# State space layer of a four-layer decoder: order of its first unit, one square root for two norms

## The chip, the cores and the metric

The kernel runs on one core of a Trainium2 chip. Its time is device microseconds from launch to end of one execution. Three runs of the kernel before are given with their median; one further execution was profiled, and it has a time of its own. Engines are called by their names or, in tables and profile lines, PE (TensorE's matmuls), PEld (its weight loads), DVE (VectorE), ACT (ScalarE), POOL (GpSimd) and SP (the sync engine, which issues DMAs).

## The reference, cut to what matters

The program is a decoder of four layers on 16 sequences of 128 tokens of width 256. Each layer adds an attention or state space part, a cross attention and an MLP to x, each on a layer norm of x. The change lies in layer 2's first part, a state space model that runs forward (`f`) and backward (`b`) over a sequence. The layer norm stands outside it and an RMS norm inside:

```
h   = (x - mean) / sqrt(var + eps)              # layer norm of x
xn  = rmsnorm(h, norm_w)                        # h * rsqrt(mean(h*h) + eps) * norm_w
z, xBC, dt = split(xn @ in_w.T)                 # 512 + 768 + 8 columns, per direction
dt  = softplus(dt + dt_bias)
xBC = silu(conv(xBC) + conv_b)                  # four taps over time, per channel
y   = ssd(xs, dt, -exp(A_log), B, C) + xs * D   # scan in chunks of 128 tokens
y   = rmsnorm(y * silu(z), gnorm_w) @ out_w.T
x   = x + h + concat(y_f, y_b) @ out_w_blk.T + out_b_blk
```

Since mean(h) is 0, mean(h*h) is var / (var + eps). So both norms of a token come from one variance.

## The kernel before, in words

All of x stays on the core as four groups `x[0]` to `x[3]` of four sequences each (128 partitions are the tokens of one sequence, 4 x 256 columns). Layers are written one after the other. A tile framework orders most instructions on each engine's queue; those given to `keep_in_program_order` (`pin`, and `pinned`, `pinned_transpose`) stay among themselves, on each engine, in the order in which the code issues them. Each engine takes its queue in order. Where two instructions touch one buffer, the later waits for the earlier through a semaphore.

PSUM buffers come from two pools: `b1` (one bank, 128x512 float32, four of them in rotation) and `b2` (two banks, two in rotation). A tile waits until the readers of the one that had its buffer before are through.

The layer before in time is layer 1's MLP (`l1_ffn`). It runs in 16 steps, one per sequence. ScalarE does per step a gate (L1217, silu), a rounding (L1253) and two evacuations of transposes (`yT`, L1235); VectorE a product (L1222), a maximum (L1091), small operations and the addition to x (L1245). Once a group of x is complete, the next layer's row operations on it can start in between.

`l2_attn` (L1266) does the following, in the order of the code:

- Weights are loaded and scaled, constants made, among them `na` (L1289, an exponential).
- `tokens(g)` (L1316 to L1338) makes the rows of one group: `bn_stats` and `bn_aggr` (L1323, L1324) for mean and variance; `rsqrt` (L190: a ScalarE square root, L191, and a VectorE reciprocal, L192) for `rs`; the normalised rows `h` (L1327, four operations); `ss` from var and `rs` (L1332, L1333) and a second `rsqrt`; x plus h (L1335); h scaled by `ss` on ScalarE (L1337, four operations); and `hidden_T`, eight TensorE transposes into two b1 tiles `tr` (L183), whose copies `hT` go to VectorE (L110) and ScalarE (L112) by turns. These transposes are not pinned.
- A `Unit` is one group in one direction; there are eight. For it `channel(u, ch)` computes 128 of the 768 columns of xBC for 512 tokens: two products into a b1 tile `xBC`, a ScalarE scaling (the last tap with bias), three VectorE taps (`stt`) that read the same b1 tile, all into `xs`. `silu(u, ch)` is applied in place by ScalarE, `gate(u, c)` makes 128 columns of z with its silu. ScalarE's operations of these have the line L1342, VectorE's L1346.
- The code before issues `tokens(0)`, then for each of six channels the channel and at once its silu, then four gates, then `tokens(1)` to `tokens(3)`.
- dt's chain follows (L1541 to L1575). Eight narrow products per all four groups go to one b1 tile, ScalarE copies it (`dT`, L1546), four transposes turn it (`dtt`), VectorE adds the bias (L1555), ScalarE does Abs, Exp and, later, Ln (L1561, L1562, L1568), and VectorE the rest, ending with `da` = A * dt (L1572, L1575).
- `sums(u)` takes cumulative sums of `da` on TensorE (`cs`), and VectorE and GpSimd make `left` and `right` from them.
- `pw` (L1577 on) is the product of both output projections, 16 products in 8 b1 tiles, each read by VectorE (L1584).
- The loop over eight units starts with `decays` of unit 0, whose first products go to two b2 tiles `seg`. In the loop, each unit's channels, gates and sums are issued one unit ahead, beside the work of the unit before it.

Functions that use a different activation table on ScalarE (square root, silu, Exp, Ln) have an ACT_TABLE_LOAD in front of them wherever the table changes.

Of the kernel before, what the change touches and what calls it, by code (L numbers as in the profile page):

```python
# [8 lines left out]
F = mybir.dt.float32  # L9
BF = mybir.dt.bfloat16  # L10
U32 = mybir.dt.uint32
AF = mybir.ActivationFunctionType
ALU = mybir.AluOpType
# [3 lines left out]
P = 128  # L17
# [4 lines left out]
NG = 4  # L22
GB = B // NG
GT = GB * P
EPS = 1e-5
# [4 lines left out]
class Decoder:  # L30
# [1235 lines left out]
    def l2_attn(self):  # L1266


        nc = self.nc
# [12 lines left out]
        with self.tc.tile_pool(name="l2a", bufs=1) as wk:  # L1282
# [28 lines left out]
            for i, d in enumerate(dirs):  # L1311
                nc.gpsimd.tensor_copy(wdt[:, :, NH * i : NH * i + NH], wx[d][:, :, CH : CH + NH])

            hTs = []

            def tokens(g):  # L1316

                h = self.hp.tile([P, GB, DM], F, tag="h", name="h", bufs=2)
                st = self.small([P, GB, 6], "bnst")
                mv = self.small([P, GB, 2], "bnmv")  # L1320
                rs = self.small([P, GB], "rstd")
                for t in range(GB):
                    nc.vector.bn_stats(st[:, t, :], self.x[g][:, t, :])  # L1323
                    nc.vector.bn_aggr(mv[:, t, :], st[:, t, :])  # L1324
                self.rsqrt(rs, mv[:, :, 1])
                for t in range(GB):
                    nc.vector.tensor_scalar(  # L1327
                        h[:, t, :], self.x[g][:, t, :], mv[:, t, 0:1], rs[:, t : t + 1], ALU.subtract, ALU.mult
                    )

                ss = self.small([P, GB], "ss")
                nc.vector.tensor_tensor(ss, mv[:, :, 1], rs, ALU.mult)  # L1332
                nc.vector.tensor_tensor(ss, ss, rs, ALU.mult)  # L1333
                self.rsqrt(ss, ss)
                nc.vector.tensor_tensor(self.x[g], self.x[g], h, ALU.add)  # L1335
                for t in range(GB):
                    nc.scalar.activation(h[:, t, :], h[:, t, :], AF.Copy, scale=ss[:, t : t + 1])  # L1337
                hTs.append(self.hidden_T(h))  # L1338


            pin = self.tc.keep_in_program_order
# [15 lines left out]
            def channel(u, ch):  # L1357

                ps = self.b1("xBC")
                for k in range(2):  # L1360
                    self.pinned(ps, wx[u.d][:, k, ch * P : (ch + 1) * P], hTs[u.g][:, k, :], start=k == 0, stop=k == 1)
                x = u.xs[:, ch, :]
                cw, cbias = self.c(f"L2_{u.d}_conv_w"), self.c(f"L2_{u.d}_conv_b")
                w = lambda k: cw[:, ch * 4 + k : ch * 4 + k + 1]
                act(x, ps, AF.Identity, scale=w(3), bias=cbias[:, ch : ch + 1])
                x3, p3 = (v.rearrange("p (t n) -> p t n", t=GB) for v in (x, ps))
                for n in range(1, 4):
                    late, early = slice(n, P), slice(0, P - n)
                    dst, src = (late, early) if u.d == "f" else (early, late)
                    stt(x3[:, :, dst], p3[:, :, src], w(3 - n), x3[:, :, dst], ALU.mult, ALU.add)  # L1370

            def silu(u, ch):
                act(u.xs[:, ch, :], u.xs[:, ch, :], AF.Silu)

            def gate(u, c):
                ps = self.b1("z")
                for k in range(2):
                    self.pinned(ps, wz[u.d][:, k, S(c)], hTs[u.g][:, k, :], start=k == 0, stop=k == 1)
                act(u.z[:, c, :], ps, AF.Silu)

            def sums(u):

                ps = self.b1("cs")[:, 0:P]
                for t in range(GB):
                    self.pinned(ps[R(t), :], da[:, u.i, u.g * GB + t, :], upto[u.d], start=True, stop=True)
                u.left = wk.tile([P, P], F, tag="left", name="left", bufs=2)
                cs = wk.tile([P, P], F, tag="cs", name="cs", bufs=2)
                u.right = wk.tile([P, NH, P], F, tag="right", name="right", bufs=1)
                yield
                ts(u.left, ps, kind[:, 1:2], kind[:, 0:1], ALU.mult, ALU.add)  # L1390
                ts(cs, ps, kind[:, 0:1], kind[:, 1:2], ALU.mult, ALU.add)
                nc.gpsimd.tensor_tensor(
                    u.right,
                    cs.unsqueeze(1).to_broadcast([P, NH, P]),
                    each.unsqueeze(2).to_broadcast([P, NH, P]),
                    ALU.mult,
                )
                yield
# [129 lines left out]
                stt(x, ps, u.rs[:, t : t + 1], x, ALU.mult, ALU.add)  # L1528


            tokens(0)
            u = Unit(0)
            for ch in (4, 5, 0, 1, 2, 3):
                channel(u, ch)
                silu(u, ch)
            for c in range(4):
                gate(u, c)
            for g in range(1, NG):
                tokens(g)

            ps = self.b1("dt")  # L1541
            for g in range(NG):
                for k in range(2):
                    self.pinned(ps[R(g), :], wdt[:, k, :], hTs[g][:, k, :], start=k == 0, stop=k == 1)
            dT = wk.tile([P, GT], F, tag="sq", name="dT", bufs=2)
            nc.scalar.copy(dT, ps)  # L1546
            ps = self.b1("dtt")
            for t in range(GB):
                self.pinned_transpose(ps[:, S(t)], dT[:, S(t)])

            dt = wk.tile([P, 2, B, NH], F, tag="dt", name="dt")
# [19 lines left out]
            for i in range(2):  # L1571
                nc.vector.tensor_tensor(  # L1572
                    da[:, i, :, 0:NH], dt[:, i], na[:, i, :].unsqueeze(1).to_broadcast([P, B, NH]), ALU.mult
                )
                nc.vector.tensor_scalar(da[:, i, :, NH : 2 * NH], da[:, i, :, 0:NH], -1.0, None, ALU.mult)  # L1575
            for _ in sums(u):
                pass  # L1577

            pw = wk.tile([P, 2, 4, DM], F, tag="pw", name="pw")
            for i, d in enumerate(dirs):  # L1580
                for c in range(4):
                    ps = self.b1("pw")[:, 0:DM]
# [5 lines left out]
            for m in range(M):  # L1588
# [56 lines left out]
                last, u = u, after  # L1645
# [765 lines left out]
```

## Time and profile before

| what | value |
|---|---|
| three runs | 3664.17, 3664.07, 3657.71 us; median 3664.07 |
| the profiled execution | 3659.25 us, its span 3657.5 us |
| mean granted TensorE clock | 0.949 |
| PE, DVE, ACT, POOL busy, share of the span | 91%, 58%, 39%, 12% |
| first xBC product starts | 1716.30 us |
| first `dt` product starts | 1751.68 us |
| `cs` starts | 1763.84 us |
| first `pw` product starts | 1764.42 us |
| first `seg` product starts | 1773.07 us |
| TensorE busy from 1716 to 1773 us | 35.43 of 57 us |
| VectorE, ScalarE busy there | 30.63 and 27.01 us |

A line of a timeline gives start, duration, engine, line of the code, operation, output and inputs with their shapes, how many instructions were merged, and in brackets how long the engine had stood before it and what it waited for last. A line of the busy table gives a stretch, its length, then busy time and number of instructions of PE, PEld, DVE, ACT and POOL, TensorE's granted clock, the DMA engines' busy share and GB/s. A duration of a merged line runs to the end of the last instruction; neighbours on TensorE overlap, so starts are the better measure of its pace.

### The profile page before, as it was taken

The numbers are of one execution on the slowest core, as the hardware profiler recorded it, in microseconds if no ns is written. First come the engines' busy times: TensorE is split into PE (matmuls) and PEld (weight loads), VectorE is DVE, ScalarE is ACT, GpSimd is POOL, SyncE is SP. The second block draws the span as 40 slices with busy tenths as digits, with TensorE's granted clock in tenths as the row PEclk, the third lists the DMA queues.
The fourth block names the chain that finished last, engine by engine and source line by source line (L and its number), as shares of the span: only waits on it lengthen the run. The fifth ranks groups of instructions, "written<-read, shape, count | busy, mean of one in ns | idle before, by whom it ended". The sixth has DMA issues, their size and how long they took to land.

```text
span 3657.5 us, 51423 instructions
## 1 busy us (share of the span) xinstructions
PE 3343.9 (91%) x20959; PEld 1806.8 (49%) x20976; DVE 2115.8 (58%) x4133; ACT 1426.7 (39%) x1917; POOL 457.2 (12%) x627
## 2 busy tenths in 40 slices
PE   7888999999998899997799999196999999999999
PEld 4655555555556556664455567062122222224656
DVE  6545444444463534468677644425799999973440
ACT  2344411111124422238455422023477777783221
POOL 5423100000003311110010110104100000002100
PEclk9978999999999999999999999597799999999989
DMA  3000000000110100010000001273312020000000
GB/s 98 4 7 1 14 20 20 18 22 18 32 48 2 38 1 1 1 42 8 12 1 12 2 1 34 105 250 107 60 25 31 11 31 11 11 1 25 1 8 18
DMA packets 90484, 105.46 MB, mean 29 GB/s; under 512 B 11364, under 2 KB 72678, under 8 KB 89990
## 3 DMA queue, kind: packets, MB, share of 16 engines
q1 hardware_dynamic: 79672, 89.71, 9.3%
q0 software_dynamic: 4224, 6.43, 0.5%
q10 hardware_dynamic: 6352, 6.03, 0.5%
q8 instruction: 165, 2.70, 0.3%
q14 instruction: 71, 0.58, 0.1%
HBM read 85.53 MB, written 16.60 MB: 28 GB/s over the span
## 4 chain that ended last, share of the span: by engine, by line
PE 79%; DVE 10%; ACT 5%; issue 3%; POOL 2%; DMA 1%; SPq 0%; POOLq 0%; ACTq 0%; DVEq 0%
PE acc L1943 7%; PE down L255 6%; PE gate L255 6%; PE up L255 6%; PE proj L255 6%; PE st L1943 5%; PE one L1943 4%; PE qT L166 4%; PE st L255 4%; PE o L255 2%; PE h L255 2%; DVE mx L2089 2%; PE rb L255 2%; PE v L948 2%; PE pr L166 2%
## 5 line engine op out<-in xcount | busy, mean ns | idle before, releaser
L2089 DVE TENSOR_REDUCE mx<-one 128x1 f32<-128x512 f32 x1024 | 659.0, 686 | 61.8 <-PE one L1943 52.7
L2226 ACT ACTIVATE e<-st 128x1024 f32<-128x1024 f32 x512 | 497.0, 1021 | 214.1 <-PE st L1943 213.0
L674 ACT ACTIVATE gs<-gate,cols 128x512 f32<-128x512 f32 x132 | 90.7, 687 | 552.6 <-PE gate L255 552.6
L1943 PE MATMUL acc<-e,v 128*32 128x512 f32 x2048 | 288.9, 613 | 0.9 <-ACT e L2226 0.9
L1943 PE MATMUL st<-qp,kp 113*128 113x512 bf16 x1024 | 273.8, 388 | 3.4 <-ACT e L2226 1.9
L688 DVE SCALAR_TENSOR_TENSOR x<-down,w_all,x 128x256 f32<-128x256 f32 x512 | 212.4, 477 | 111.1 <-PE down L255 110.9
L255 PE MATMUL down<-expert,gs 128*128 128x256 f32 x1056 | 251.0, 381 | 2.2 <-DVE gs L675 2.2
L255 PE MATMUL gate<-hT,expert 128*128 128x512 f32 x528 | 250.3, 596 | 0.0
L255 PE MATMUL up<-hT,expert 128*128 128x512 f32 x528 | 248.7, 593 | 0.0
L255 PEld LDWEIGHTS down<-expert,gs 128*128 128x128 f32 x1056 | 201.5, 191 | 86.1 <-issue 61.5
L675 DVE SCALAR_TENSOR_TENSOR gs<-up,cols,gs 128x512 f32<-128x512 f32 x132 | 99.0, 750 | 229.8 <-PE up L255 229.8
L1943 PE MATMUL one<-kp,qp 16*128 16x512 bf16 x1024 | 211.7, 399 | 4.0 <-DVE mx L2089 2.6
L1943 PEld LDWEIGHTS <-qp 16*128 16x128 bf16 x1024 | 49.0, 91 | 332.4 <-issue 327.0
L255 PEld LDWEIGHTS up<-hT,expert 128*128 128x128 f32 x528 | 100.8, 191 | 127.1 <-issue 126.9
L1943 PEld LDWEIGHTS <-kp 113*128 113x128 bf16 x1024 | 79.1, 98 | 141.8 <-issue 81.8
L1048 ACT COPY rb<-rb 128x512 f32<-128x512 f32 x64 | 37.5, 586 | 258.9 <-PE rb L255 258.9
L255 PEld LDWEIGHTS gate<-hT,expert 128*128 128x128 f32 x528 | 100.4, 192 | 70.5 <-issue 64.0
L1050 DVE TENSOR_TENSOR cT<-o,rb 128x512 f32<-128x512 f32 x64 | 44.3, 692 | 157.0 <-ACT rb L1048 157.0
L166 PE MATMUL qT<-hT,L_xattn_Wq 128*128 128x512 f32 x256 | 115.8, 606 | 6.6 <-DVE hT L110 4.5
L1346 DVE SCALAR_TENSOR_TENSOR xs<-xBC,cols,xs 128x508 f32<-128x508 f32 x144 | 106.1, 742 | 22.4 <-ACT xs L1342 19.0
L255 PE MATMUL o<-e,v 128*32 128x128 f32 (+1 forms) x2048 | 105.7, 280 | 11.8 <-DVE nm L292 11.8
L962 POOL CAST kb<-kT 128x512 bf16<-128x512 f32 x64 | 41.5, 677 | 433.9 <-DVE kT L110 433.9
(519 smaller groups left out, 5507.9 us busy)
## 6 DMA issues: line engine op xcount, KB each, us to landing
W<-in_L_ffn_W_dram SPq DMA_DIRECT2D x46, 512.0 KB, 5.5
expert<-in_L_ffn_Wg_dram SPq DMA_DIRECT2D x32, 128.0 KB, 2.2
expert<-in_L_ffn_Wu_dram SPq DMA_DIRECT2D x32, 128.0 KB, 2.7
expert<-in_L_ffn_Wd_dram SPq DMA_DIRECT2D x32, 128.0 KB, 2.4
parts<-parts SPq DMA_DIRECT2D x16, 256.0 KB, 2.3
qp<-parts SPq DMA_DIRECT2D x28, 128.0 KB, 3.8
kp<-parts SPq DMA_DIRECT2D x12, 256.0 KB, 8.3
hs<-zero SPq DMA_DIRECT2D x23, 128.0 KB, 1.9
```

Source lines behind the costliest of these rows:

```text
L166: self.nc.tensor.matmul(out, lhsT, rhs, start=i == 0, stop=i == n - 1 and bias is None)
L255: self.tc.keep_in_program_order(self.nc.tensor.matmul(*a, **k))
L674: nc.scalar.activation(gs, pg, AF.Silu, bias=bg)
L675: nc.vector.scalar_tensor_tensor(gs, pu, bu, gs, ALU.add, ALU.mult)
L688: nc.vector.scalar_tensor_tensor(xt, pd[:, t, :], w_all[:, o : o + 1], xt, ALU.mult, ALU.add)
L948: nc.tensor.matmul(ps, l, r, start=True, stop=False)
L962: nc.gpsimd.tensor_copy(kb[:, i + j, :], kT[:, i + j, :])
L1050: nc.vector.tensor_tensor(cT, po, rb, ALU.mult)
L1346: stt = lambda *a: pin(nc.vector.scalar_tensor_tensor(*a))
L1943: self.tc.keep_in_program_order(nc.tensor.matmul(*a, **k))
L2089: nc.vector.tensor_reduce(mx[:, t, kc, i : i + 1], pair[i], AX.X, ALU.max)
L2226: nc.scalar.activation(e[:, 2 * p : 2 * p + 2, :], ps, AF.Exp, scale=1.0 / 16.0)
```

## The change

`tokens(g)` is split. `rows(g)` does the row operations, and both roots are taken by one ScalarE operation: with a = 1/(var + eps), `rs` is sqrt(a), and `ss` is sqrt(1/(var*a + eps)). VectorE makes both arguments with five small operations, and no reciprocal follows the root. `turn(g)` does the eight transposes, now pinned, and the two copies. The issue order becomes: rows 0 and 1, turn 0, rows 2, channel 4, channel 5 and silu 4, turn 1 and rows 3, channel 0, silu 5, turn 2, channel 1, silu 0, turn 3; then dt's products, copy and transposes with channel 2 and silu 1 between them, in b2 tiles instead of b1; the rest of dt's chain; then channel 3, silu 2, gate 0, silu 3, gates 1 to 3, and the sums. `pw` and the loop over units are as they were.

The orders of the queues differ only in one stretch ahead of `seg`: on TensorE from the end of the MLP's `down` products to `cs`, on VectorE and ScalarE from the first group's rows (in the MLP's second half) to `left` and to the load of the table for the decays. ScalarE has seven instructions fewer, VectorE four more. The queues of GpSimd and the sync engine are in the same order in both.

```diff
-            def tokens(g):
+            def rows(g):
...
-                rs = self.small([P, GB], "rstd")
+                both = self.small([P, 2, GB], "rstd2")
+                rs, ss = both[:, 0], both[:, 1]
                 for t in range(GB):
                     nc.vector.bn_stats(st[:, t, :], self.x[g][:, t, :])
                     nc.vector.bn_aggr(mv[:, t, :], st[:, t, :])
-                self.rsqrt(rs, mv[:, :, 1])
+
+                nc.vector.tensor_scalar(rs, mv[:, :, 1], EPS, None, ALU.add)
+                nc.vector.reciprocal(rs, rs)
+                nc.vector.tensor_tensor(ss, mv[:, :, 1], rs, ALU.mult)
+                nc.vector.tensor_scalar(ss, ss, EPS, None, ALU.add)
+                nc.vector.reciprocal(ss, ss)
+                nc.scalar.activation(both, both, AF.Sqrt)
...
-                ss = self.small([P, GB], "ss")
-                nc.vector.tensor_tensor(ss, mv[:, :, 1], rs, ALU.mult)
-                nc.vector.tensor_tensor(ss, ss, rs, ALU.mult)
-                self.rsqrt(ss, ss)
                 nc.vector.tensor_tensor(self.x[g], self.x[g], h, ALU.add)
...
-                hTs.append(self.hidden_T(h))
+                hs[g] = h
+
+            def turn(g):
+                hT = self.hp.tile([P, 2, GT], F, tag="hT", name="hT", bufs=5)
+                for k in range(2):
+                    ps = self.b1("tr")
+                    for t in range(GB):
+                        self.pinned_transpose(ps[:, t * P : (t + 1) * P], hs[g][:, t, k * P : (k + 1) * P])
+                    self.evac(hT[:, k, :], ps)
+                hTs.append(hT)
...
-            tokens(0)
+            rows(0)
+            rows(1)
+            turn(0)
+            rows(2)
             u = Unit(0)
-            for ch in (4, 5, 0, 1, 2, 3):
+            chs = (4, 5, 0, 1, 2, 3)
+            for k, ch in enumerate(chs[:4]):
                 channel(u, ch)
-                silu(u, ch)
-            for c in range(4):
-                gate(u, c)
-            for g in range(1, NG):
-                tokens(g)
-
-            ps = self.b1("dt")
+                if k:
+                    silu(u, chs[k - 1])
+                if k == 1:
+                    turn(1)
+                    rows(3)
+                if k > 1:
+                    turn(k)
+
+            ps = self.b2("dt")[:, 0:GT]
...
             nc.scalar.copy(dT, ps)
-            ps = self.b1("dtt")
+            channel(u, chs[4])
+            silu(u, chs[3])
+            ps = self.b2("dtt")[:, 0:GT]
...
+            channel(u, chs[5])
+            silu(u, chs[4])
+            gate(u, 0)
+            silu(u, chs[5])
+            for c in range(1, 4):
+                gate(u, c)
             for _ in sums(u):
                 pass
```

More of the change, by code (lines that the diff above doesn't have):

```diff
@@ L1312, in l2_attn @@
                 nc.gpsimd.tensor_copy(wdt[:, :, NH * i : NH * i + NH], wx[d][:, :, CH : CH + NH])
-            hTs = []
-            def tokens(g):
+            hs, hTs = {}, []
+            def rows(g):
                 h = self.hp.tile([P, GB, DM], F, tag="h", name="h", bufs=2)
```

## The prediction

> **What bounds the kernel now.** I read the page first (TensorE busy 91% of 3657.5 us, but only 70% in the two slices from 1646 to 1829), then busy time by stretch of the few stages that the diff touches, the waits of TensorE there, and the timelines of the engines one by one. The stretches show an MLP tail (to 1716) that is bound by ScalarE, and a front of the state space layer (1716 to 1764) in which no engine is full: columns are stretch, length, then busy time of PE, weight loads, DVE, ACT, POOL, then TensorE's clock.
>
> ```profile
> 1680.00:1700.00 20.00, 18.84 (x125) 12.26 (x126) 18.82 (x36) 20.00 (x27) 1.41 (x5) 1.00 0.01 2
> 1700.00:1716.00 16.00, 9.98 (x73) 6.82 (x71) 11.99 (x35) 15.75 (x24) 1.06 (x5) 1.00 0.12 36
> 1732.00:1744.00 12.00, 6.65 (x15) 2.34 (x15) 6.69 (x9) 4.72 (x9) 0.00 (x0) 1.00 0.00 0
> 1744.00:1764.00 20.00, 8.75 (x51) 4.65 (x53) 9.41 (x20) 10.73 (x18) 0.00 (x0) 0.84 0.00 0
> ```
>
> So the front is a chain of handovers. Its first half is a ping-pong between two queues: ScalarE's silu of one channel waits for VectorE's three taps of it, and the first step of the next channel stands behind that silu. A channel costs 3.73 us (31.77 to 35.49) although the taps take only 2.30.
>
> ```profile
> 1731.77 0.63 ACT L1342 ACTIVATE xs<-xs 128x512 f32<-128x512 f32 x1 [2.43 <-DVE xs L1346]
> 1732.30 0.76 ACT L1342 ACTIVATE xs<-xBC,cols 128x512 f32<-128x512 f32 x1
> ...
> 1735.49 0.63 ACT L1342 ACTIVATE xs<-xs 128x512 f32<-128x512 f32 x1 [2.43 <-DVE xs L1346]
> ```
>
> Its second half is dt's chain, alone: TensorE stands in order before the sums `cs`, and only then can the pw products and the first unit's decays (`seg`) start.
>
> ```profile
> 1751.68 3.42 PE L255 MATMUL dt<-hT,wdt 128*32 128x512 f32 x16
> 1755.78 0.66 PE L258 MATMUL dtt<-ident,dT 128*128 128x128 f32 x4 [0.68 <-ACT dT L1546]
> 1763.84 0.65 PE L255 MATMUL cs<-tri_up,da 128*32 128x128 f32 x8 [7.41 <-DVE da L1575]
> 1764.42 8.81 PE L166 MATMUL pw<-L_wbT,out_w 128*128 128x256 f32 x32
> 1773.07 1.03 PE L255 MATMUL seg<-never_f,identb 128*128 128x512 bf16 x4
> ```
>
> From the first xBC matmul (1716.30) to `seg` (1773.07) is 56.8 us, of which TensorE stood for 21.3 (the sum of its gaps). From `seg` on, the order of every queue is the same in both programs; GpSimd's and the DMA queue's orders do not change at all. So what counts is when `seg` starts.
>
> In the MLP tail, each group's two square roots cost two table loads and often two back:
>
> ```profile
> 1667.04 1.28 ACT L191 ACT_TABLE_LOAD   x1
> 1668.33 0.30 ACT L191 ACTIVATE rstd<-bnmv,eps 128x4 f32<-128x4 f32 x1
> 1668.65 1.28 ACT L1217 ACT_TABLE_LOAD   x1
> ...
> 1674.36 1.28 ACT L191 ACT_TABLE_LOAD   x1
> 1675.66 0.30 ACT L191 ACTIVATE ss<-ss,eps 128x4 f32<-128x4 f32 x1
> ...
> 1678.25 1.28 ACT L1217 ACT_TABLE_LOAD   x1
> ```
>
> **What the Trainium skill says.** "ScalarE: Activation LUTs", section "What ACT_TABLE_LOAD costs", gives 1283 ns for a load and a further 1380 ns of drain. The trace agrees on the load (1.28) and not on the drain: the root starts 0.01 us after it. I use 1.28. "TensorE: Matmul & The Clock Gate", section "What's actually happening", says that an idle window of about 3.4 us halves the clock. The trace agrees: after the 7.41 us wait the clock was 0.62 and 0.53 (1760 to 1768), after gaps of 3.00 and below (1724 to 1744) it stayed 1.00, after 3.16 it was 0.84 and 0.74 (1748 to 1756). "PSUM — Partial Sum Buffer", section "PSUM: the matmul accumulator", has eight banks; the kernel's four b1 and two double b2 buffers are all of them. Moving dt and dtt to b2 therefore leaves the b1 rotation (transposes, channels, gates) four deep; which b1 buffer comes free when is the wait I watch below.
>
> **The change, part by part.** I use the clock of the trace before and drop its "17". Durations: three taps 2.27 with handover; channel's ACT step 0.76, silu 0.55 to 0.63, hT half 0.68 on DVE and 0.57 on ACT; a channel or gate on TensorE 1.78, a group's eight transposes 1.0 (1.91 for sixteen).
>
> *One root for both norms.* In the MLP tail ScalarE has 7 loads and 5 roots before, 5 loads and 3 roots after: 2 x 1.28 + 2 x 0.30 = 3.2 us less. VectorE gets one small operation more a group (five where four were, 0.15 to 0.2 each). All of the load gain lies at group 0, between the gate step at 1663.11 and the one at 1682.83. Following the new queues with the same durations, the gate step that started at 1682.83 starts at 1680.5; VectorE, full there (23.47 of 25 us), and the wait for qy eat 0.7. At the end the third load (1.28 + 0.30) now stands right before the last two yT; most of that lies beside their eight transposes, and I charge 0.2. Gain 2.1; bounds 0 (VectorE binds) to 3.2.
>
> *Front.* First channels (xB4, xB5) leave TensorE as before, 16.3 to 19.9, turn(1) to 20.9. On ScalarE the four scalings of group 2's rows are queued ahead of both channel steps and wait for VectorE's x+h (19.1): 19.2 to 20.9, so channel 4 is read at 20.9 and not at 18.3. That is a new wait, of 2.6. Taps of channel 4 end at 24.0, of channel 5 at 26.9 (four row operations of group 3, 0.35 each, stand between them, and wait for ScalarE's root at 24.6). Channel 0's matmuls need channel 4's b1 buffer: 24.1 to 25.9. turn(2) needs channel 5's buffer: 27.0 to 28.0. Then on ScalarE hT, channel 0's step (29.65), four scalings of group 3 (31.45, waiting for x+h at 29.65), channel 1's step (32.2); taps of channel 0 to 31.95; turn(3) 32.05 to 33.0; taps of channel 1 to 35.75. dt's eight products 33.05 to 36.3 (3.42 measured at a clock of 0.74 to 0.84; I take 3.2), channel 2 to 38.1, dtt to 38.75, channel 3 to 40.5, gates 0 to 2 to 45.9.
>
> *dt's chain beside the channels.* dt's add at 39.0 to 39.5, taps of channel 2 to 41.75 (they hide abs, load, exp on ScalarE to 41.7 and the load of ln), then the long VectorE run to da, 4.65 as in the trace before: 46.4. Channel 3's taps stand behind it: 48.65. Gate 3 needs channel 3's b1 buffer: 48.75 to 50.55. The sums cs stand behind gate 3 in TensorE's written order: 51.2. What is late at the end is thus VectorE (dt's run, then the taps) and through a buffer TensorE, not ScalarE, whose silus, gates and the load for exp end at 52 under the pw products. The 7.41 wait turns into 2.9 (45.85 to 48.75).
>
> *pw.* Warm, 8 x 0.87 = 6.95 (0.87 is VectorE's measured beat on them), after a cold start 8.7: `seg` at 58.2 or 59.9. The 2.9 gap lies just under those that stayed at 1.00. I take warm, plus 1.2 for some thirty handovers that I set at 0 to 0.1 where the trace shows about 0.04 to 0.1: `seg` at 59.4, 13.7 earlier than 73.07. Bounds: 8 to 18.
>
> *Silu one channel later* has no cost of its own: xs is in SBUF and silu's reader comes later. dt and dtt in b2 cost nothing: the MLP's last use of b2 (VectorE's gate product at 1705) is over, and seg takes them after 58. ScalarE's loads in the front go from eight to seven (a root's and its way back to silu less, silu's after ln more); it is not last there.
>
> Sum: 2.1 + 13.7 = 15.8 us. The profiled execution took 3659.25 (span 3657.5, 1.75 around it), so it would be 3643.5. The median of the three runs shown is 3664.07, 4.8 above it; from the median 3648.3. I give 3648.
>
> **Rivals.** (a) *New waits in the written orders eat half.* The scalings ahead of the channel steps and the b1 chain (channel 4's taps, channel 0, channel 5's taps, turn(2)) are computed at best case; if each of the four turns waits 2 us longer, the gain is 15.8 - 8 = 8, time 3656. For it: the front becomes one interleaved chain through four buffers. Against: each engine has slack (counted from the new queues, DVE has about 29 us of work and ACT about 25, in 42). (b) *TensorE near its floor.* Its own work in the front is 34.5 us (channels and gates 17.8, transposes 4, dt 3.4, dtt and cs 1.3, pw 8); were waits shorter than I make them, with 2 us for the first transposes' way `seg` could come at 16.3 + 36.5 = 52.8, 20 earlier; with the MLP's 2 the time is 3664 - 22 = 3642. Against: da cannot come before dt's run, which needs all four groups. (c) *The change doesn't do what it says:* da is earlier but `seg` is not, since VectorE's taps and rows only move in front of it; gain 0 to 3, 3662. Against: VectorE stood for 4.2 + 2.2 us in dt's chain and 1.4 in every channel. (d) *Slower: the clock.* From 24 on the new order spreads about 28 us of TensorE work over gaps of 1.1, 2.3 and 2.9. Should the clock fall there to the 0.53 measured at 1764 and stay, that work costs 28 / 0.53 - 28 = 25 us more, 6 of it inside the waits, and half of the first unit's 13.1 us (1775 to 1790) starts cold as well, +6: 25 - 6 + 6 - 15.8 = +9, time 3673. It ends slower than before once about two thirds of this work is cold. Against: gaps of 1.8 to 3.0 in 1724 to 1744 left the clock at 1.00.
>
> **How the numbers follow.** Forecast, 3643 to 3654: 0.65. (a), 3652 to 3660: 0.15. (b), 3636 to 3643: 0.10. (c): 0.06. (d): 0.04. A measurement of this kernel tells about 0.2% (7.3 us) from no change. Faster by more than that (below 3656.7): the forecast, (b) and half of (a), 0.82; within it 0.14; slower 0.04. The range, 3638 to 3658, holds the forecast (its own ends include the bounds of pw's clock and of the MLP tail), 0.11 of (a) and 0.07 of (b), 0.83 in all.
>
> **What would show it.** One ScalarE root a group on 128x8; five loads in the MLP tail; `seg` 42 to 45 us after the first xBC matmul (56.8 before); first channel step about 2.6 us later than before; dt's products before channel 2, and a wait of gate 3 on the taps of about 3 us in place of the 7.4 before cs; pw at 0.87 a piece. The prediction is wrong if the distance from `seg` to the end of the kernel changes, if TensorE's clock in the front falls below 0.9, or if the four-buffer waits exceed 3.3 us.

## The result, and the profile after

| | before | after |
|---|---|---|
| five runs, us | 3651.47, 3657.71, 3659.58, 3664.07, 3664.17 | 3629.88, 3631.07, 3632.91, 3635.93, 3646.33 |
| median, us | 3659.58 | 3632.91 |
| profiled execution, us (span) | 3659.25 (3657.5) | 3646.33 (3644.6) |
| its mean TensorE clock | 0.949 | 0.948 |

The ratio is 0.9939 [0.9922, 0.9956], 22.3 us faster at 3659.6 (the two medians differ by 26.7). The forecast was 3648 with a range of 3638 to 3658: the sign held, and the time fell 5 us below the range. The profiled execution after is the slowest of its five, so the two profiles differ by only 12.9 us. Compared stage by stage, they nevertheless show the whole gain of the changed code. I cut both at three points: the ScalarE gate step from which the MLP tail was counted (1663.11 before, 1668.43 after), the first xBC product (1716.30, 1719.49) and `seg` (1773.07, 1759.68).

| stage, us | before | after | change | forecast |
|---|---|---|---|---|
| start to the gate step | 1663.11 | 1668.43 | +5.3 | 0 |
| MLP tail: gate step to first xBC | 53.19 | 51.06 | -2.1 | -2.1 |
| front: first xBC to `seg` | 56.77 | 40.19 | -16.6 | -13.7 |
| `seg` to the end of the span | 1884.4 | 1884.9 | +0.5 | 0 |

The two middle rows are 18.7 us. The 5.3 us ahead of them belong to instructions that are the same, in the same order, in both kernels.

First the busy time by stretch of the kernel after; columns as in the prediction (stretch, length, PE, weight loads, DVE, ACT, POOL, TensorE's clock, DMA share, GB/s).

```profile
1685.80:1719.50 33.70, 27.40 (x187) 17.86 (x185) 28.69 (x75) 32.87 (x46) 2.47 (x10) 1.00 0.06 19
1719.50:1734.90 15.40, 11.27 (x40) 5.58 (x40) 13.80 (x30) 10.57 (x20) 0.00 (x0) 1.00 0.01 4
1734.90:1741.40 6.50, 6.50 (x30) 2.82 (x30) 4.25 (x9) 4.00 (x8) 0.00 (x0) 1.00 0.00 0
1741.40:1751.80 10.40, 8.29 (x17) 2.90 (x15) 7.69 (x15) 7.72 (x11) 0.00 (x0) 0.89 0.01 2
```

The MLP tail is still ScalarE's (32.87 of 33.70 us). In the front TensorE is now busy 33.95 of 40.19 us where it was 35.50 of 56.77, and its clock there is 0.96.

The front's first half on ScalarE's timeline (start, duration, engine, line, operation, count, and in brackets the wait):

```profile
1722.30 1.70 ACT L1339 ACTIVATE h<-h,rstd 128x256 f32<-128x256 f32 x4 [2.70 <-DVE x L1337]
1723.91 1.43 ACT L1353 ACTIVATE xs<-xBC,cols 128x512 f32<-128x512 f32 x2
1725.23 0.57 ACT L112 COPY hT<-tr 128x512 f32<-128x512 f32 x1
1725.82 1.28 ACT L1332 ACT_TABLE_LOAD   x1
1727.12 0.21 ACT L1332 ACTIVATE rstd<-rstd 128x8 f32<-128x8 f32 x1
1727.34 1.28 ACT L1353 ACT_TABLE_LOAD   x1
1728.64 0.63 ACT L1353 ACTIVATE xs<-xs 128x512 f32<-128x512 f32 x1
1729.17 0.57 ACT L112 COPY hT<-tr 128x512 f32<-128x512 f32 x1
```

The 2.43 us waits of each silu for its own taps are gone: both channel steps run back to back (1.43 for two), and the silu of channel 4 comes 4.7 us after its channel step, 1.6 us after its taps are through (1727.01 on VectorE). The group 2 scalings stand ahead and wait 2.70 us, the new wait that the prediction named.

TensorE's timeline from channel 0 to `seg`:

```profile
1724.41 1.98 PE L255 MATMUL xBC<-hT,L_f_wx 128*128 128x512 f32 x4 [0.35 <-DVE hT L110]
...
1727.06 0.66 PE L258 MATMUL tr<-ident,h 128*128 128x128 f32 x4 [0.23 <-DVE xs L1357]
1729.80 1.99 PE L255 MATMUL xBC<-hT,L_f_wx 128*128 128x512 f32 x4 [2.08 <-ACT hT L112]
1733.04 1.96 PE L258 MATMUL tr<-ident,h 128*128 128x128 f32 x8 [1.26 <-ACT h L1339]
1734.93 2.55 PE L255 MATMUL dt<-hT,wdt 128*32 128x512 f32 x16
...
1748.81 3.08 PE L255 MATMUL z<-hT,L_f_wz 128*128 128x512 f32 x4 [2.11 <-ACT z L1353]
1751.83 0.66 PE L255 MATMUL cs<-tri_up,da 128*32 128x128 f32 x8
1752.41 7.43 PE L166 MATMUL pw<-L_wbT,out_w 128*128 128x256 f32 x32
1759.68 1.03 PE L255 MATMUL seg<-never_f,identb 128*128 128x512 bf16 x4
```

`cs` no longer waits: the 7.41 us have become 2.11 us in front of gate 3 and nothing behind it. The first product of dt comes 15.44 us after the first xBC, where it came 35.38 after it.

The first root of the MLP tail, on ScalarE:

```profile
1677.38 1.28 ACT L1332 ACT_TABLE_LOAD   x1
1678.68 0.21 ACT L1332 ACTIVATE rstd<-rstd 128x8 f32<-128x8 f32 x1
...
1681.19 1.28 ACT L1217 ACT_TABLE_LOAD   x1
```

One root on 128x8 (0.21) stands where two on 128x4 (0.30 each) stood, and the group takes one load and one back. From the gate step at 1668.43 to the one at 1685.77 are 17.34 us, where there were 19.72.

### The profile page after: what moved, and what is told of

Same layout as the page of the kernel before. It is cut to its first block, busy times and chain, and to the rows that moved or that the text cites. A ratio compares the mean times of both kernels' runs of the same rounds, so it can differ in the third digit from the quotient of the medians.

```text
span 3644.6 us, 51429 instructions
## 1 busy us (share of the span) xinstructions
PE 3348.9 (92%) x20976; PEld 1807.7 (50%) x20976; DVE 2113.7 (58%) x4137; ACT 1421.1 (39%) x1910; POOL 456.9 (13%) x627
## 4 chain that ended last, share of the span: by engine, by line
PE 79%; DVE 10%; ACT 5%; issue 3%; POOL 2%; DMA 1%; SPq 0%; POOLq 0%; ACTq 0%; DVEq 0%
PE acc L1968 7%; PE down L255 6%; PE gate L255 6%; PE up L255 6%; PE proj L255 6%; PE st L1968 5%; PE one L1968 4%; PE qT L166 4%; PE st L255 4%; PE o L255 2%; PE h L255 2%; DVE mx L2114 2%; PE rb L255 2%; PE v L948 2%; PE fc L166 2%
```

## The experiments

**The theory and its rivals.** The theory after the result: the changed stretch is worth 18.7 us, of which the single root gives the MLP's 2.1 and the order the front's 16.6; the rest of the difference between single executions is TensorE's clock in code that is the same. Rivals: the single root also shortens the front; the written (pinned) order as such is what helps; and, called P in the expectations, the change moves the later stages against the windows in which the clock is granted, so that a steady part of the gain lies behind `seg`. In the tables, "stretch" runs from the gate step to `seg` (109.96 before).

All kernels compute everything that the reference asks for. The stages of all profiles are in one table; "half-clock" is the time between the first xBC and `seg` during which the records show TensorE at half its clock. Times of kernels in the right column are medians, of as many executions as stand in brackets, from four sessions; ratios are against executions of before in the same session.

| kernel | gate step at | MLP tail | front | half-clock in front | stretch | `seg` to end | time, us |
|---|---|---|---|---|---|---|---|
| before | 1663.11 | 53.19 | 56.77 | 10.2 | 109.96 | 1884.4 | 3659.58 (5) |
| before again | 1672.03 | 53.16 | 56.84 | 13.7 | 110.00 | 1876.0 | 3658.40 (14) |
| after | 1668.43 | 51.06 | 40.19 | 3.4 | 91.25 | 1884.9 | 3632.91 (5) |
| after again | 1671.22 | 51.06 | 40.20 | 3.4 | 91.26 | 1871.0 | 3635.72 (8) |
| after, third | 1660.82 | 51.06 | 40.13 | 3.4 | 91.19 | 1877.7 | 3631.57 (11) |
| root only | 1659.49 | 51.04 | 56.24 | 10.2 | 107.28 | 1886.1 | 3648.34 (22) |
| order only | 1663.89 | 53.20 | 38.11 | 3.4 | 91.31 | 1874.6 | 3635.46 (7) |
| silu later only | 1660.79 | 53.16 | 49.54 | 13.7 | 102.70 | 1883.8 | 3649.04 (1) |
| dt late | 1666.30 | 51.04 | 47.98 | 13.7 | 99.02 | 1869.7 | 3636.70 (1) |
| not pinned | 1659.44 | 51.04 | 41.52 | 6.8 | 92.56 | 1877.3 | 3631.00 (1) |
| `na` late | 1669.56 | 51.06 | 39.23 | 0.0 | 90.29 | 1878.9 | 3640.43 (1) |
| pw spread | 1668.37 | 51.04 | 41.03 | 3.4 | 92.07 | 1877.3 | 3641.84 (22) |
| pw spread, `na` late | 1660.31 | 51.04 | 45.12 | 13.7 | 96.16 | 1876.9 | 3634.71 (16) |
| pw piece twice | 1664.95 | 51.05 | 41.92 | 3.4 | 92.97 | 1871.0 | 3636.57 (22) |

### How far two executions of one kernel differ

The kernel before, unchanged, and the changed kernel, unchanged, twice more.

> The kernel before, once more, with a profile of its own. Theory L (local): the whole gain of the change lies between the MLP's gate step that started at 1663.11 us before the change (1668.43 after) and the first seg product: 18.7 us in the two profiles shown, 2.1 of it in the MLP's tail and 16.6 in the front; what the medians show beyond that (26.7 us) is TensorE's granted clock in other stages, which differs from one execution to the next. Then this profile shows 109.0 to 111.0 us from that gate step to seg, 56 to 57.5 us from the first xBC product to seg, but stretches ahead of it and after seg that differ from the first profile by some us in either direction, together with the clock. Rival D (downstream): the change makes the stretch after seg shorter in most executions, and the profile shown of the changed kernel (3646.33, the slowest of its five) was an exception. Then seg to the end here is 1884 us again and it is shorter by 5 to 8 in the next kernel.

> The changed kernel once more. Theory L: gate step to seg 91 to 92.5 us, first xBC to seg 40 to 41 us, as in its first profile; the time against the kernel before, over enough rounds, goes to -18.7 us (ratio 0.9949) and the clock of single executions explains the rest. Rival D: ratio near 0.9925 (-27 us) again, and in the profile seg to the end is 5 to 8 us under the 1884.4 of before.

> The changed kleinel a third time for more executions (13 so far: -23.4 us, with an interval of 4.4, against 57 of the kernel before). In the profiles, gate step to seg is 91.25 and 91.26 (before: 109.96 and 110.00), 18.7 us less. Theory L, all gain in this stretch: the mean over all executions goes to about -19. Rival P: the change also shifts where the rest of the program falls in the clock's windows (seg starts 0.8 to 0.9 us after a window's edge in both profiles of before, 2.2 and 2.4 in those of the changed kernel), and the rest gains about 4 us on average: the mean stays near -23.

Measured against the kernel before run beside them: before again 0.9998 [0.9983, 1.0014]; after again 0.9935 [0.9912, 0.9957]; after a third time 0.994 [0.992, 0.9959]. The stretch repeats to 0.1 us in both kernels. The parts that are the same code do not: the gate step lies between 1659.4 and 1672.0, and `seg` to the end takes 1869.7 to 1886.1. All executions of before in this study (116) have a mean of 3656.7 and a standard deviation of 7.2 us; all of the changed kernel (24) a mean of 3633.8 and 6.75. So the gain is 22.9 +/- 3.0 us, 18.7 of it in the changed stretch; in the three sessions with several executions of both it was 24.2, 23.7 and 22.5. That is the size which the last expectation gave to rival P, and not the -19 of theory L; whether P is the cause is asked below, with the pw piece done twice. The three runs of before that the prediction was built on had a median 7.4 above the mean of 116.

That the front repeats does not mean that it ran alike. In the first two profiles of the changed kernel gate 3 took 3.08 and 3.23 us and dt 2.55; in the third it was dt:

```profile
1727.33 4.08 PE L255 MATMUL dt<-hT,wdt 128*32 128x512 f32 x16
...
1742.73 1.98 PE L255 MATMUL z<-hT,L_f_wz 128*128 128x512 f32 x4 [2.11 <-ACT z L1353]
1744.64 0.43 PE L255 MATMUL cs<-tri_up,da 128*32 128x128 f32 x8
1745.00 7.17 PE L166 MATMUL pw<-L_wbT,out_w 128*128 128x256 f32 x32
```

Each of the three had one stretch of 3.41 us at half clock; it fell on gate 3 and `cs` in two and on dt in this one, and cost about 1.5 us in either place (from dt to the next product 4.01 us instead of 2.48).

### The single root alone, and the order alone

Root only keeps `rows`' arithmetic and the old order; order only is the changed kernel with the old roots.

```diff
 # order only, against the changed kernel
-                both = self.small([P, 2, GB], "rstd2")
...
-                nc.scalar.activation(both, both, AF.Sqrt)
+                rs = self.small([P, GB], "rstd")
+                self.rsqrt(rs, mv[:, :, 1])
...
+                nc.vector.tensor_tensor(ss, ss, rs, ALU.mult)
+                self.rsqrt(ss, ss)
```

> The kernel before with nothing but one root for both norms. By the prediction's sum the MLP's tail gains 2.1 us; in the front the two roots' switch of tables (1724.24 and 1726.75, 2.6 us with the root) goes, of which at most 2 lie on the way. Theory L: -2 to -5 us, and the 18.7 is not made here. If the root were the main cause: -10 or more.

> The changed kernel with the two roots of before put back, so the order alone. Theory L: the front keeps most of its 16.6 us, the MLP's tail loses its 2.1, and the second switch of tables for group 3 now stands in ScalarE's queue ahead of the channels: -11 to -16 us against before. If root and order need each other (the order's queues wait for the second root): -8 or less.

Root only: MLP tail -2.1, front -0.5 (together 2.7, as expected), time 0.9983 [0.9974, 0.9993]. Order only: MLP tail as before, front 38.11, time 0.995 [0.993, 0.9971]; with 18.7 us off the stretch it gained more than the 11 to 16 expected. The front of order only is 2.1 us shorter than with the single root, and its MLP tail 2.1 longer, so its stretch (91.31) equals the changed kernel's (91.25). The single root's worth inside the whole change is thus nothing that these runs show: 2.1 won in the MLP tail is given back in the front. This rests on one profile of order only. The place is between turn 2 and dt. In order only TensorE's timeline reads:

```profile
1726.60 0.66 PE L258 MATMUL tr<-ident,h 128*128 128x128 f32 x4 [1.66 <-DVE hT L110]
1727.25 3.19 PE L255 MATMUL xBC<-hT,L_f_wx 128*128 128x512 f32 x4
1730.23 1.56 PE L258 MATMUL tr<-ident,h 128*128 128x128 f32 x8
```

Channel 1 and turn 3 follow without a wait, where the changed kernel waits 2.08 and 1.26. Channel 1 starts hardly earlier for that (10.16 us after the first xBC, against 10.31), since turn 2 waits longer (1.66, against 0.23), and it ran partly at half clock (3.19). But dt starts at 14.63 instead of 15.44. When gate 3 starts, order only is 0.5 us ahead and has paid for its half-clock window; the changed kernel pays for its own only then, on gate 3 and `cs`. Group 3's scalings, which turn 3 needs, ran 8.2 us after the first xBC, on ScalarE's timeline of order only:

```profile
1724.13 0.30 ACT L191 ACTIVATE ss<-ss,eps 128x4 f32<-128x4 f32 x1
1725.29 1.71 ACT L1337 ACTIVATE h<-h,ss 128x256 f32<-128x256 f32 x4 [0.86 <-DVE ss L192]
1726.90 0.76 ACT L1351 ACTIVATE xs<-xBC,cols 128x512 f32<-128x512 f32 x1
1727.68 1.28 ACT L1351 ACT_TABLE_LOAD   x1
```

In the changed kernel they ran 13.0 us after it (1732.50), and group 3's root with its load and the load back to silu (1725.82 to 1728.64) stands on ScalarE between its copy `hT` of turn 1 and its copy `hT` of turn 2 (1729.17), for which channel 1 waits. So the two kernels differ in where the tile framework places group 3's rows among the taps, besides the root itself; which of the two costs the 2.1 was not taken apart.

### Silu one channel later, alone

```diff
 # against the kernel before
-            for ch in (4, 5, 0, 1, 2, 3):
+            for k, ch in enumerate(chs):
                 channel(u, ch)
-                silu(u, ch)
+                if k:
+                    silu(u, chs[k - 1])
+            silu(u, chs[5])
```

> The kernel before with silu issued one channel later, and nothing else. If the ping-pong of ScalarE and VectorE cost what the first half of the front shows (3.73 us a channel against 2.27 for the taps), four to five channels get 1.4 us shorter each: first xBC to seg 56.8 - 6 = 50 to 51.5 us. If the rows' roots and table loads among the channels are the true limit there, 54 us or more.

The front took 49.54, 7.2 us less than before and 0.5 below the expected range. TensorE's timeline:

```profile
1713.95 10.57 PE L255 MATMUL xBC<-hT,L_f_wx 128*128 128x512 f32 x24 [1.18 <-DVE hT L110]
...
1739.81 1.64 PE L183 MATMUL tr<-ident,h 128*128 128x128 f32 x8 [3.16 <-ACT h L1337]
1741.37 3.94 PE L255 MATMUL dt<-hT,wdt 128*32 128x512 f32 x16
...
1754.06 0.66 PE L255 MATMUL cs<-tri_up,da 128*32 128x128 f32 x8 [7.42 <-DVE da L1578]
1754.64 9.01 PE L166 MATMUL pw<-L_wbT,out_w 128*128 128x256 f32 x32
```

The six channels follow without a gap, and everything behind keeps its waits: 3.16 before the last turn and the 7.42 before `cs`. Undoing the ping-pong of two in-order queues is worth 7.2 us by itself, for a line of code.

### dt's chain back behind the gates

```diff
 # against the changed kernel: ahead of dt's products
+            channel(u, chs[4])
+            silu(u, chs[3])
+            channel(u, chs[5])
...
+            for c in range(1, 4):
+                gate(u, c)
```

> The changed kernel with dt's whole chain (products to da) moved back behind the gates. In the kernel before the chain took 12.2 us from its first product to cs; here it would start about when gate 3 is issued. Theory: first xBC to seg 46 to 48 us in place of 40.2, so that about 6 to 8 of the 16.6 come from dt's chain lying beside the channels and the rest from the channels' order. If dt's place were nearly all of it: 52 us or more. If the chain's VectorE part only moved (rival c of the prediction): 41 or less.

```profile
1745.03 1.94 PE L255 MATMUL dt<-hT,wdt 128*32 128x512 f32 x16
1747.70 0.66 PE L258 MATMUL dtt<-ident,dT 128*128 128x128 f32 x4 [0.74 <-ACT dT L1571]
1755.68 0.66 PE L255 MATMUL cs<-tri_up,da 128*32 128x128 f32 x8 [7.32 <-DVE da L1600]
1756.27 9.22 PE L166 MATMUL pw<-L_wbT,out_w 128*128 128x256 f32 x32
```

The front took 47.98, 7.8 us longer than with the chain beside the channels. The wait of 7.32 before `cs` is back (the changed kernel has 2.11 in its place), and behind it pw runs at half clock for much of its length: 9.22 where it took 7.43, so that 1.8 of the 7.8 come through the clock. So 7.2 for the silus and 7.8 for dt's place make 15.0 of the 16.6. The remaining 1.6 lies between this kernel (47.98) and silu later only (49.54), whose half-clock times are equal: the rest of the order and the single root, which I did not take apart.

### The transposes not pinned

```diff
-                        self.pinned_transpose(ps[:, t * P : (t + 1) * P], hs[g][:, t, k * P : (k + 1) * P])
+                        nc.tensor.transpose(ps[:, t * P : (t + 1) * P], hs[g][:, t, k * P : (k + 1) * P], self.ident)
```

> The changed kernel with its 32 transposes left to the scheduler, as before. The order on TensorE comes out the same but for the first transpose, which moves in between two down products. Theory: first xBC to seg 40.2 within 0.3, so that the written order of TensorE as such is worth nothing here. If it counted, 1 us or more.

```profile
1720.79 3.58 PE L255 MATMUL xBC<-hT,L_f_wx 128*128 128x512 f32 x4 [2.08 <-ACT hT L112]
...
1727.20 4.19 PE L255 MATMUL dt<-hT,wdt 128*32 128x512 f32 x16
```

The expectation of the front's length missed: 41.52. TensorE's order is the same but for the first group's transposes, and the milestones are equal up to channel 1, 10.31 us after the first xBC. There channel 1 took 3.58 (1.99 pinned) and dt 4.19 (2.55): this execution had two half-clock windows in the front, the pinned ones one. With 1.5 us a window, an estimate from the runs above, the two are equal. Writing the transposes' order by hand is worth nothing that this run shows; only the transposes were tested so, the channels and taps were pinned in every kernel.

### The load for `na` out of the way

I thought that channel 1's wait came from ScalarE changing its table to the exponential for `na` (L1289) just ahead of the front, so that group 3's root had to load its own table again. Here `na` is made later, next to dt's exponential.

```diff
-            nc.scalar.activation(na.rearrange("p a h -> p (a h)"), self.b("L2_A_log"), AF.Exp)
-            nc.vector.tensor_scalar(na, na, -1.0, None, ALU.mult)
...
+            act(na.rearrange("p a h -> p (a h)"), self.b("L2_A_log"), AF.Exp)
+            nc.vector.tensor_scalar(na, na, -1.0, None, ALU.mult)
```

> The changed kernel with na's exponential moved beside dt's exponential, so that the square root's table is not displaced between group 2's root and group 3's: two loads (2.57 us) fewer on ScalarE ahead of and in the front. In the changed kernel with two roots the front was 2.1 us shorter (38.1) than with one (40.2), and I put this down to this reload, which holds group 3's root, rows and turn back. Theory: 38 to 39 us from first xBC to seg, with the MLP's 51.06 kept. If the single root's longer VectorE chain ahead of it is the cause: 40 us.

The theory fell. ScalarE's timeline has the root without a load ahead of it:

```profile
1726.35 0.57 ACT L112 COPY hT<-tr 128x512 f32<-128x512 f32 x1
1726.82 0.21 ACT L1330 ACTIVATE rstd<-rstd 128x8 f32<-128x8 f32 x1
1728.39 1.28 ACT L1351 ACT_TABLE_LOAD   x1 [1.36 <-DVE xs L1355]
```

It comes 6.20 us after the first xBC instead of 7.63. Turn 3 nevertheless starts at 13.48 instead of 13.55: group 3's rows stand among and behind the taps on VectorE's queue, whatever the root does:

```profile
1727.58 1.39 DVE L1355 SCALAR_TENSOR_TENSOR xs<-xBC,cols,xs 128x500 f32<-128x500 f32 x2
1728.88 0.41 DVE L1332 TENSOR_SCALAR h<-x,bnmv,rstd 128x256 f32<-128x256 f32 x1
...
1730.83 0.41 DVE L1332 TENSOR_SCALAR h<-x,bnmv,rstd 128x256 f32<-128x256 f32 x1
1731.15 0.69 DVE L110 COPY hT<-tr 128x512 f32<-128x512 f32 x1
```

The front's 39.23 is 1.0 less than the changed kernel's, but it is the only one without any half-clock window. With 1.5 taken off for one window the changed kernel would need 38.7, so this edit brings nothing. Its dt took 3.25 at full clock (2.55 in the changed kernel): VectorE's copy `hT` of turn 3, which dt reads, stood behind four taps (1733.68 to 1736.60) instead of three.

### The pw products in the gaps

If what is left in TensorE's waits can be filled with pw, whose 7.4 us stand last ahead of `seg`, the front should come down to 35 to 37. The first run spreads the pieces over the front, pinned, in one b2 tile a direction; the second also makes `na` late.

```diff
+            weights(0, (0,))
...
+                    if k == 3:
+                        weights(0, (3,))
+                if k == 2:
+                    weights(0, (1, 2))
...
+                if c == 3:
+                    weights(1, range(4))
```

> The changed kernel with its eight pw pieces (7.3 us between cs and seg, waiting for nothing but weights) moved into TensorE's waits: one before channel 4, two before channel 1, one before turn 3, four before gate 3, in b2 tiles. TensorE stood there for about 7 us in the front. Theory: first xBC to seg 35 to 37 us (40.2 before), time 4 us under the changed kernel's. If VectorE, which gets the eight readings among its taps, is the limit: 39 us or more.

> The same, with na's exponential beside dt's, so with two table loads fewer in the front. On its own that moved group 3's root 1.4 us earlier but not its rows, which stand behind taps in VectorE's queue. Theory: within 1 us of the kernel with pw spread alone (35 to 37 us from first xBC to seg).

41.03 and 45.12: both expectations of a gain fell, and neither kernel beats the changed one (0.9966 [0.9952, 0.998] and 0.9949 [0.9931, 0.9967] against before). The first is slower than it, by 9.0 +/- 4.2 us in the mean of all executions; its stretch (0.8 longer) and the new wait of 1.9 shown below account for 2.7 of that, and the rest stays open. The waits of TensorE in the first, by what they waited for (in total, times, longest):

```profile
PE pw L255 <- DVE pw L1356: 7.5, 4, 3.8
```

The pieces ahead of gate 3 on its TensorE timeline, and the second set of `seg` products:

```profile
1753.89 1.13 PE L255 MATMUL pw<-L_wbT,out_w 128*128 128x256 f32 x4 [2.55 <-DVE pw L1356]
1755.60 1.13 PE L255 MATMUL pw<-L_wbT,out_w 128*128 128x256 f32 x4 [0.58 <-DVE pw L1356]
...
1763.34 1.14 PE L255 MATMUL seg<-right,left 32*128 32x512 f32 x8 [1.86 <-POOL right L1403]
```

Each next piece of a pair or four, written in order on TensorE and into the same b2 tile, waits for the reading of the one before. The first such wait of each set (3.84 and 2.55) ends with a reading that stood behind rows or taps in VectorE's queue. In the two short ones (0.58 each) VectorE was not busy: it stood 1.23 us before each of these readings, waiting for the piece. In the changed kernel each piece has a b1 tile of its own, and pw runs without a wait. So the shared tile costs by itself, and that VectorE is the limit, as the rival had it, is not shown; spread pieces in tiles of their own were not tried.

The last line shows a second thing. `cs` goes through VectorE and a GpSimd operation (`right`, 1.89 us) before `seg`'s second set of products can start. In the changed kernel pw fills that time, and the set starts 0.96 us after the first `seg` product; here it starts 2.90 after it. Moving pw away thus opened a new wait behind the point where the front is cut, and 41.03 flatters this kernel by 1.9 us.

The second kernel has the same waits (7.2) and the same new wait of 1.86, but four half-clock windows in its front where the first has one, and its gate 3 took 3.17. Its front lies 4.1 us from the first's, where within 1 was expected.

### One pw piece twice

For rival P: the changed kernel with a quarter of pw's products repeated, which only moves everything behind it by some 1.7 us against the clock's windows.

```diff
-                for c in range(4):
+                for c in (0, 0, 1, 2, 3):
```

> The changed kernel with the first pw piece of each direction computed twice, so 2 x 0.87 = 1.7 us of TensorE work more right before seg, and nothing else. Theory L: gate step to seg 93.0, and the mean 1.7 us above the changed kernel's. Rival P: seg falls half a window later, and the rest of the program changes by some us: the mean is off that value by 4 us or more, to either side.

The stretch was 92.97, as expected, and the mean of 22 executions 3636.45, against 3633.8 of the changed kernel: +2.7 +/- 4.0, which agrees with the 1.7 us of added work. A shift of 4 us beyond that lies just inside the interval, so P is neither shown nor excluded. By the edges in the clock's records `seg` starts 1.9 us after one in both profiles of before, within 0.5 us of one in the three of the changed kernel, and 1.6 us after one here (the figures in the expectation of the third run of the changed kernel are not these). So this edit put `seg` nearly where it lies in the kernel before.

## Why the prediction was wrong, step by step

Three terms failed: the reference point (7.4 us), the front, where the chain through b1 buffers that set its pace was not there (2.9), and what lies outside the changed stretch, put at nothing (4.2 +/- 3.0). The last one's cause stays open.

**The reference point.** The sum, -15.8, was set against 3664.07, the median of three runs. The prediction noted that the profiled execution was 4.8 below it and still took the upper one. The mean of 116 executions is 3656.7: 7.4 of the 15.1 us by which the forecast missed the median of five.

**One root.** "Gain 2.1; bounds 0 to 3.2": measured 2.1 in the tail, and two loads and two roots fewer there, as counted. What the prediction left out is the root in the front, charged at nothing ("it is not last there"): order only's front is 2.1 shorter, with group 3's root and rows standing earlier in both queues.

**Front.** 13.7 was forecast, 16.6 measured, inside the bounds of 8 to 18. Start of each step in us after the first xBC:

| step | forecast | measured |
|---|---|---|
| first channel step on ScalarE | 4.6 | 4.42 |
| channel 0 | 7.8 | 4.92 |
| turn 2 | 10.7 | 6.74 |
| channel 1 | 11.7 | 10.31 |
| turn 3 | 15.75 | 13.55 |
| dt | 16.75 | 15.44 |
| channel 2 | 20.0 | 17.92 |
| `dtt` | 21.8 | 19.74 |
| `da` done | 30.1 | 27.97 |
| taps of channel 3 done | 32.35 | 30.18 |
| gate 3 | 32.45 | 29.32 |
| `cs` | 34.25 | 32.34 |
| pw | 34.9 | 32.92 |
| `seg` | 43.1 | 40.19 |

The first step that failed is "Channel 0's matmuls need channel 4's b1 buffer". They did not: channel 0 waited 0.35 us for a copy `hT`, the reading of turn 1's first tile. In strict rotation it would have had channel 4's buffer, which was read until 1727.01. The framework did not keep to rotation: turn 2's second tile got that buffer (it waited 0.23 for the taps), and channel 1 one of turn 2's. So the chain of buffers that set the forecast's pace for 8 us was not there. Most of that came back, at channel 1 (2.08 for a copy `hT` behind the root's loads, which the forecast had set as harmless) and at turn 3 (1.26 for the scalings). Left of it at dt's start are 1.3 us. dt itself took 2.5 instead of 3.2, since it ran at full clock: 0.8. From `dtt` to `da` the forecast had 8.3 and the trace 8.23, and channel 3's taps behind it 2.25 and 2.21: that part of the working was exact. Gate 3 again took another buffer, that of gate 0, free 0.9 us before channel 3's taps ended (1749.67):

```profile
1747.38 2.29 DVE L1357 SCALAR_TENSOR_TENSOR xs<-xBC,cols,xs 128x508 f32<-128x508 f32 x3
```

Against all that, gate 3 and pw ran partly at half clock (1.5 us more than forecast). The 1.2 us set aside for handovers were not needed. Together: 1.3 + 0.8 + 1.0 - 1.5 + 1.2 = 2.8 of the 2.9.

**dt's chain.** Right as a mechanism: `cs` stands behind gate 3 and no longer for `da`; 2.11 in place of the forecast's 2.9, released by gate 0's evacuation and not by the taps.

**pw.** 7.27 us to `seg` against 7.0: at full clock but for the first 0.6 us, 0.87 a piece.

**`seg` to the end.** "Shouldn't change" holds for the order of instructions, and for the pair of profiles (+0.5). It is no test, though: the same code took 1869.7 to 1886.1 us. The mean gain of 22.9 +/- 3.0 exceeds the stretch's 18.7 by 4.2 +/- 3.0. By subtraction this lies outside the changed stretch. It goes with TensorE's clock: the mean over executions was 0.9496 before and 0.9520 after, and over the executions of before 0.001 of clock goes with about 2.9 us. Some 0.001 of that rise is the front's own, whose half-clock time fell from 10.2 or 13.7 to 3.4 us; what is left of it would be about 4 us, an estimate. Whether the change causes that through the phase of the clock's windows stays open: root only, whose `seg` lies as before, also has 3.4 us more than its stretch explains (6.1 +/- 2.2 against 2.7). The piece done twice leaves as much, 3.3 +/- 3.3, although its `seg` lies elsewhere in the window; order only leaves 0.7 +/- 5.1, and pw spread lacks 4.0 +/- 3.5.

**The range.** It held the bounds of the stages and none for the execution. A standard deviation of 7 us in code that nobody touched has to be in it. Stages, reference point and rest make 3648.3 - 7.4 - 2.9 - 4.2 = 3633.8, the mean after (the 4.2 is what was left over, so the sum has to close); the median of five is 0.9 lower.

**The rivals.** (b), "TensorE near its floor", named the right direction and the number (`seg` at 36.5 after the first xBC) was too low by 3.7. TensorE's own work was reckoned well (34.5, measured 33.95); its waits were 6.2 us and not 2, above all 2.08 before channel 1, 1.26 before turn 3 and 2.11 before gate 3. (a) and (c) are refuted by the stage table. (d): one half-clock window fell in the front, costing 1.5 us, not 25.

## What to carry to other kernels

Where an in-order engine must wait for another engine's work on tile k, put its work on tile k+1 ahead of the wait: here that alone was worth 7.2 us of a front of 57. Start a long chain of small operations (dt's, 8 us) as soon as its inputs exist and let wide work run beside it; then ask what the chain's waits turn into, since most of 7.4 us was won and 2.1 remained. Before moving work out of a stretch, ask what it covers there: pw stood between `cs` and `seg`, but hid 1.9 us of GpSimd's wait. Judge an edit of 0.5% by the distance between two events of its own stage, which repeated to 0.1 us here as long as the same number of half-clock windows fell into it (one more cost 1.3 us), while the whole time of one execution has a standard deviation of 7 us; and set the forecast against a mean of many runs.

## What the runs showed of the hardware

TensorE's granted clock changes in the records only at the edges of a grid 3.413 us wide, and is either 1.0 or 0.5. The grid lies differently against the kernel's start in each execution. This is what the Trainium skill, "TensorE: Matmul & The Clock Gate", section "What's actually happening", says of a free-running window of 3413 ns; every profile here agrees. The prediction took from this section that an idle window halves the clock, and found the trace of before in agreement. That holds only in part: the window ahead of the first half-clock one was not idle. TensorE was busy for 0.86 of its 3.41 us in the kernel before (1747.30 to 1750.71), and for 1.31 in the changed one (1746.14 to 1749.56). The busy time of that one window doesn't decide either: with 1.60 and 1.64 us (1733.64 to 1740.47, before) the clock stayed at 1.0, and with 2.03 (1724.26 to 1727.68, the changed kernel's third profile) it fell.

The same section puts the penalty of the warm-up below 1% of a typical kernel and advises against fitting a count of slow matmuls. The clock of 0.949 in the kernel before stands for some 373 of 3657 us at half clock. Between executions the time moved by only 0.2% (7 us), and yet by the size of the effect that was to be measured. What I had not expected is that the same waits were followed by half clock in some executions and not in others: behind the wait of 2.08, channel 1 ran at 1.99 in the pinned kernel and at 3.58 in the unpinned one; behind that of 2.11, gate 3 took 3.08 and 3.23 in two profiles of the changed kernel and 1.98 in the third.
